# The last gate and routing ahead of the early experts, and the first batches' tables summed at the last scan's start

## The chip, the cores and the metric

One core of a Trainium2 chip runs the kernel. The metric is the device time in microseconds (us) of one execution; the kernel before took 2051.53 us, the median of three runs.

## The reference

The input x has 4 batches of 512 tokens of width 512. Four residual blocks follow each other. The last two are what the change is about: a state-space scan that is gated by the layer-normed x, and a mixture of experts over all 2048 tokens together.

```python
x = x + _L0_xattn_ref(_layernorm(x), fside, ctx)            # eight int8-quantised expert forwards
x = x + _L0_ffn_ref(_layernorm(x), lut, gate_idx, ...)      # dense FFN, weights looked up in a table of 16
x = x + _L1_xattn_ref(ctx, _layernorm(x), ...)              # scan over time, 512 channels x 16 states, times silu(z)
x = x + _L1_ffn_ref(_layernorm(x), gate_w, w_gate, w_up, w_down)   # mixture of experts
...
probs = softmax(x @ gate_w); w, sel = top_k(probs, 8); w = w / sum(w)
order = argsort(flat_e); pos = arange(P) - start[se]
slot = where(pos < C, se * C + pos, E * C)                  # C = 1024 slots for each of 32 experts
xg = x_pad[t_slot].reshape(E, C, H)
y = (silu(xg @ w_gate) * (xg @ w_up)) @ w_down
out = zeros((T + 1, H)).at[t_slot].add(w_slot[:, None] * y)
```

A token goes to 8 of 32 experts, and within an expert it takes the next free slot in token order. So an expert's list of slots needs the routing of all tokens that it is to work on.

## The kernel before

**Stages.** Weights of the second block are decoded first, woven with the first block. Then, for each batch b of 4, a scan (`scan`, lines 537 to 589) is woven with the second block's matmuls (`lut_ffn`), with `prepare` of the next batch, and with the gate and the routing of batch b-1. After the last scan, eight "early" experts (numbers 0 to 7) run over the tokens of batches 0 and 1. Then the PSUM banks are laid out anew, and 32 "late" expert calls follow: experts 8 to 31 over all tokens with 576 slots each, and experts 0 to 7 over batches 2 and 3 with 320 slots each. At the end two sums are added to x and written out.

**The order of the work.** The framework keeps a tile's buffers in pools. An instruction waits until its operands are there and until its output's buffer is free. Each engine runs its own instructions in a fixed order that follows the order of the program. `weave` takes steps of several generators in turn, in proportion to their given counts, and so sets that order; `chain` runs one generator after another, `run` runs one to its end. `pipeline` lets three experts overlap: while one is in its second matmul, the next is in its first, and the one after that is transposed.

**The scan.** For each of 64 groups of channels a tile `d` (tag "d", 4 buffers) is loaded by SP (L556). ScalarE makes the decay (`st`, L561), GpSimd the input term (`dBu`, L563), VectorE runs the recurrence (L566, L569), and TensorE sums over the states (`py`, L577). `BC` (L545) is loaded once for a batch. L587 ends each quarter of a scan.

**Gate and route.** `gate(b)` (L591 to L611) normalises x, multiplies with the scan's output, transposes (`pt_y`, L608), and adds to x. `route(b)` (L682 to L749) normalises x by blocks of 128 tokens (`xn_r`), stores these rows to DRAM (`xln`: one copy for the experts' gathers of batches 0 and 1, and one with all batches), transposes (`pt_r`), multiplies with the gate weights (`pl`, copied to `logits`), and takes the softmax and the best eight. `place` (L767 to L821) counts the tokens of each expert (`pp`), makes the slot numbers (`to`), and writes each token's number into its slot in a table in DRAM: 32 indirect DMAs of GpSimd for a batch (`table<-i_tok`, L814), which keep their order. There are two groups of eight tables: `tables[0]` for batches 0 and 1, `tables[1]` for 2 and 3. Within a group consecutive scatters go to different tables.

**Tables to tokens.** A slot is filled in one table of a group at most; the others hold zero there. `table_rows` (L823) loads the rows of several tables with one SP DMA for each (L835) into one tile `rows`, stacked over the partitions; with 24 experts, five tables fit on 128 partitions. `table_sum` (L841) adds the stacked tables by a matmul with a 0/1 matrix `pick` (L849 and L851 build it on VectorE from slices of the identity; L856 is the matmul). `slot_tokens` (L865) makes integer token numbers (for the gather) and row numbers (for the accumulate). The sums are named "a" (group 0, experts 0 to 7; read when the last scan begins), "u" (both groups, experts 8 to 31; read after the early experts) and "b" (group 1, experts 0 to 7; after "u").

**An expert** (`expert`, L896 to L990). SP loads its weights (`egu`, `ed`: 3 buffers each). GpSimd gathers its rows by indirect DMA (`xg`, L918, 10 buffers, blocks of 128; an early expert has 128, 128 and 64). TensorE transposes them (`pt_g`, L931), ScalarE and VectorE copy them (`exT`, L933), and ScalarE copies the routing weight of each row (`gates`, L934). Then come the first matmul (`pg`, L943), the activation (`eh`: tanh on ScalarE L959, two products on VectorE L960 and L961), the second matmul (`po_e`, L972 and L976), the scaling (`ey`, 4 buffers; VectorE L983 or ScalarE L985), and an indirect DMA of GpSimd which adds the rows to a sum in DRAM (`sums<-ey`, L986). An early expert's three blocks go to two sums in turn, so its third accumulate waits until its first has landed. PSUM banks of the early stage come under the tags "t" (two banks, shared by `pt_y`, `pt_r`, `pl`, `pp`, `pt_g`, `po_e` and the tables' sums), "m" and others.

Of the kernel before, what the change touches and what calls it, by code (L numbers as in the profile page):

```python
# [16 lines left out]
F32 = mybir.dt.float32  # L17
# [5 lines left out]
ALU = mybir.AluOpType  # L23
# [4 lines left out]
P = 128  # L28
NB = 4
S = 512  # L30
# [3 lines left out]
KH = HID // P  # L34
# [7 lines left out]
NE = 32  # L42
# [6 lines left out]
SLOTS = 576  # L49
EARLY = 8  # L50
ROOM = (320, 320)
# [8 lines left out]
class Kernel:  # L60
# [554 lines left out]
    def routing_constants(self, rp):  # L615
        nc, t = self.nc, self.t
        c = rp
        self.gate_w = c.tile([P, KH, NE], F32, name="gate_w", bufs=1)
        nc.sync.dma_start(out=self.gate_w, in_=t["gate_w"].rearrange("(k p) e -> p k e", p=P))
        tri = c.tile([P, P], F32, tag="xn", name="tri", bufs=1)  # L620
        make_upper_triangular(nc, tri, 1.0, diag=False)
        self.tri = c.tile([P, P], BF16, name="trib", bufs=1)
        nc.vector.tensor_copy(self.tri, tri)
        self.ones = c.tile([P, P], BF16, name="ones", bufs=1)
        nc.vector.memset(self.ones, 1.0)

        def iota(n, step, base, mult, name):
            i = c.tile([P, n], I32, name=f"{name}_i", bufs=1)
            nc.gpsimd.iota(i, pattern=[[step, n]], base=base, channel_multiplier=mult)
            f = c.tile([P, n], F32, name=name, bufs=1)  # L630
            nc.vector.tensor_copy(f, i)
            return f

        self.i_e = iota(NE, 1, 0, 0, "i_e")
        self.i_tok = iota(NT, P, 1, 1, "i_tok")
        row = iota(1, 0, 0, 1, "i_row")
        self.chosen = c.tile([P, NT, TOPK], F32, name="chosen", bufs=1)

        self.spare = c.tile([P, 2], F32, name="spare", bufs=1)
        nc.vector.tensor_scalar(self.spare[:, 0:1], row, float(NE * SLOTS), None, ALU.add)  # L640
        nc.vector.tensor_scalar(self.spare[:, 1:2], row, float(NE * CAP), None, ALU.add)
        self.no_row = c.tile([P, 1], F32, name="no_row", bufs=1)
        nc.vector.tensor_scalar(self.no_row, row, float(NB * S + 1), None, ALU.add)
        self.more_p = c.tile([P, 1], F32, name="more_p", bufs=1)
        nc.vector.memset(self.more_p, 0.0)
        self.seen = [c.tile([P, NE], BF16, name=f"seen{g}", bufs=1) for g in range(2)]
        for seen in self.seen:
            nc.vector.memset(seen, 0.0)
# [171 lines left out]
                self.tc.keep_in_program_order(scatter)  # L820
                yield  # L821

    def table_rows(self, pool, tag, tables, n, e0, e1, m):  # L823


        nc = self.nc
        ne = e1 - e0
        per = P // ne
        parts = -(-len(tables) // per)
        r = pool.tile([P, parts, m], F32, tag=tag, name="rows")  # L830
        rows = []
        for a in range(parts):
            group = tables[a * per : (a + 1) * per]
            for i, table in enumerate(group):
                nc.sync.dma_start(  # L835
                    out=r[i * ne : (i + 1) * ne, a, :],
                    in_=table[e0 * n : e1 * n].rearrange("(e n) o -> e (n o)", n=n)[:, :m],
                )
            rows.append(r[: len(group) * ne, a, :])
        return rows  # L840

    def table_sum(self, rp, rows, e0, e1, m, name):

        nc = self.nc
        nb = -(-m // P)
        ne = e1 - e0

        pick = rp.tile([P, ne], F32, tag="pick", name="pick", bufs=1)
        nc.vector.tensor_copy(pick, self.ident[:, :ne])  # L849
        for a in range(ne, P - ne + 1, ne):  # L850
            nc.vector.tensor_tensor(pick, pick, self.ident[:, a : a + ne], ALU.add)  # L851
        pt = self.bank("t", f"pt_{name}")
        for j in range(nb):
            w = min(P, m - j * P)
            for i, r in enumerate(rows):
                nc.tensor.matmul(  # L856
                    pt[:w, j * ne : (j + 1) * ne],
                    lhsT=r[:, j * P : j * P + w],
                    rhs=pick[: r.shape[0], :],
                    start=i == 0,  # L860
                    stop=i == len(rows) - 1,
                )
        return pt[:, : nb * ne].rearrange("p (j e) -> p j e", j=nb)

    def slot_tokens(self, rp, tok, m, name):  # L865

# [185 lines left out]
def run(steps):  # L1052
    for _ in steps:
        pass
# [15 lines left out]
def weave(*streams):  # L1070

    streams = [[0, n, g] for g, n in streams]
    while streams:
        s = min(streams, key=lambda s: s[0] / s[1])
        s[0] += 1
        if next(s[2], StopIteration) is StopIteration:
            streams.remove(s)
# [3 lines left out]
def tile_kernel(ctx: ExitStack, tc: tile.TileContext, t: dict):  # L1081
    k = Kernel(tc, t)
    k.constants(ctx)
    scan = ExitStack()
    with ExitStack() as early:
        with ExitStack() as ffn:
            wp = ffn.enter_context(tc.tile_pool(name="wp", bufs=1, side="right"))
            with ExitStack() as first:
                k.banks(first, t=2, m=2, y=2, d=2)
                ap = first.enter_context(tc.tile_pool(name="ap", bufs=2))  # L1090
                sq = staggered([k.smooth_quant(ap, b) for b in range(NB)], 15)
                with ExitStack() as lut:
                    lc = lut.enter_context(tc.tile_pool(name="lc", bufs=1, side="right"))
                    lp = lut.enter_context(tc.tile_pool(name="lp", bufs=2, side="right"))
                    k.lut_tables(lc, wp)
                    lookups = k.lut_weights(lp, k.jobs)
                    weave((islice(sq, 40), 40), (islice(lookups, 48), 48))
                    k.tile_rows(wp, lc)
                    weave((islice(sq, 48), 48), (lookups, 4 * len(k.jobs) - 48), (k.scratch(lc), 4 * CHAINS))

                pp = ffn.enter_context(tc.tile_pool(name="pp", bufs=1, side="right"))
                k.scan_weights(pp)
                k.prep_tag = "y"
                preps = 2 * KH + 1
                weave((k.prepare(pp, pp, 0), preps), (sq, 30 * NB - 88))
            k.banks(early, t=2, m=2, y=1, d=3)
            k.prep_tag = "t"
            bp = ffn.enter_context(tc.tile_pool(name="bp", bufs=2, side="right"))
            rp = ctx.enter_context(tc.tile_pool(name="rp", bufs=1))
            mp = scan.enter_context(tc.tile_pool(name="mp", bufs=2))  # L1110
            k.routing_constants(rp)
            steps = (TPB // 2) * (NIC + 3)
            units = KH * 16
            routes = TPB + 2 + TPB * TOPK

            ffn_ = chain(*(k.lut_ffn(bp, b) for b in range(NB)))
            run(islice(ffn_, 4))
            for b in range(NB):
                n = steps
                streams = [(k.scan(mp, b), units), (islice(ffn_, n), n)]  # L1120
                if b + 1 < NB:
                    streams.append((k.prepare(pp, (pp, mp)[(b + 1) % 2], b + 1), preps))
                if b:
                    run(k.gate(mp, b - 1))
                    streams.append((k.route(rp, b - 1), routes))
                if b == NB - 1:
                    rows = k.table_rows(rp, "xT", k.tables[0], SLOTS, 0, EARLY, ROOM[0])
                    tok = k.table_sum(rp, rows, 0, EARLY, ROOM[0], "a")
                    at = k.slot_tokens(rp, tok, ROOM[0], "a")
                weave(*streams)  # L1130
        ep = ctx.enter_context(tc.tile_pool(name="ep", bufs=2, side="right"))
        k.expert_buffers(ep)
        full, nc = SLOTS // P, tc.nc
        two = [k.sums[j % 2] for j in range(full + 1)]
        first = k.pipeline(k.expert(ep, e, (k.xln[0], *at, 0), e, ROOM[0], two) for e in range(EARLY))
        weave((chain(k.gate(mp, NB - 1), k.route(rp, NB - 1)), KH + routes), (first, 2 * EARLY))
    scan.close()
    k.banks(ctx, t=4, g=4)
    k.gu_tag = "g"
    tp = ctx.enter_context(tc.tile_pool(name="tp", bufs=6))  # L1140
    rows = k.table_rows(ep, "exT", k.tables[0] + k.tables[1], SLOTS, EARLY, NE, SLOTS)
    at = k.slot_tokens(rp, k.table_sum(rp, rows, EARLY, NE, SLOTS, "u"), SLOTS, "u")
    rows = k.table_rows(ep, "exT", k.tables[1], SLOTS, 0, EARLY, ROOM[1])
    at_b = k.slot_tokens(rp, k.table_sum(rp, rows, 0, EARLY, ROOM[1], "b"), ROOM[1], "b")
    k.overflow(rp)
    calls = [(e, at, e - EARLY, SLOTS) for e in range(EARLY, NE)]
# [64 lines left out]
```

## Time and profile before

| what | us |
|---|---|
| runs | 2049.74, 2051.53, 2053.53 |
| median of the runs | 2051.53 |
| the profiled execution's own time | 2053.26 |
| its span in the profile | 2051.4 |
| end of the last scan (L587) | 1162.0 |
| first early expert's `pt_g` | 1170.4 |
| last add of the last gate (L610) | 1193.7 |
| first and last scatter of the last batch (L814) start | 1237.2 and 1331.1 |
| last early expert's `po_e` ends | 1314.9 |
| first late expert's `pt_g` | 1349.6 |

The profile records one execution. All points of time in this document count from the start of its span. The engines are PE (TensorE matmul), PEld (TensorE's weight load, which overlaps), DVE (VectorE), ACT (ScalarE), POOL (GpSimd) and SP (SyncE, which issues DMAs; SPq is its queue). A timeline row gives start, duration, engine, line, operation, output<-inputs and shape; the bracket tells how long the engine was idle before it and what it waited for. A row of the waits gives the total, the number and the longest.

### The profile page before, as it was taken

What the parts mean: (1) busy time and instruction counts of PE and PEld (TensorE: products, weight loads), DVE (VectorE), ACT (ScalarE), POOL (GpSimd) and SP (SyncE); (2) the same over time, 40 slices, a digit from 0 to 9 for tenths busy, and PEclk for the clock granted to TensorE, in tenths of its full rate; (3) what the DMA queues carried; (4) which work ended last, traced back from release to release, by engine and by line L of the source; (5) the groups of instructions that cost most, each with busy time, mean ns of one, the idle gap of its engine ahead of it and who ended that gap; (6) DMA issues with size and microseconds to landing.
All of it is one profiled execution on the core that took longest, in us unless ns stands there. A gap on an engine that the chain in (4) does not pass through costs nothing. (4 is left out here: it accounts for less than half of the span.)

```text
span 2051.4 us, 24293 instructions
## 1 busy us (share of the span) xinstructions
PE 1681.2 (82%) x8385; PEld 991.7 (48%) x8385; DVE 1162.8 (57%) x1986; ACT 701.0 (34%) x1329; POOL 1113.8 (54%) x952
## 2 busy tenths in 40 slices
PE   4788774998887788787868679589999999999980
PEld 2444332655554455354636244265565565665640
DVE  6888764888788779776978533132222232322331
ACT  1554347345533544353423222122222222222210
POOL 3111015668557964697569726646565556555420
PEclk9989885999998998898989789889999999999995
DMA  9433613888777778586769666658888878778655
GB/s 266 122 108 107 221 32 102 209 201 220 196 178 178 187 190 215 132 210 169 204 140 234 172 177 145 130 147 189 179 195 177 191 154 188 166 159 183 124 129 180
DMA packets 193369, 348.97 MB, mean 170 GB/s; under 512 B 46370, under 2 KB 92930, under 8 KB 193236
## 3 DMA queue, kind: packets, MB, share of 16 engines
q1 hardware_dynamic: 148932, 254.19, 46.3%
q0 software_dynamic: 44048, 92.73, 23.1%
q8 instruction: 69, 1.13, 0.2%
q14 instruction: 64, 0.52, 0.1%
q10 hardware_dynamic: 256, 0.39, 0.1%
HBM read 278.12 MB, written 77.57 MB: 173 GB/s over the span
## 5 line engine op out<-in xcount | busy, mean ns | idle before, releaser
L943 PE MATMUL pg<-exT,egu 128*128 128x320 f32 (+1 forms) x1536 | 401.7, 419 | 12.3 <-DVE eh L960 7.9
L986 POOL DMA_INDIRECT sums<-ey,to x168 | 260.6, 1551 | 276.0 <-DMA sums<-ey,to 126.7
L563 POOL TENSOR_TENSOR dBu<-d,BC 128x512 f32<-128x512 f32 x256 | 324.6, 1280 | 81.3 <-DMA d<-dts 48.0
L943 PEld LDWEIGHTS pg<-exT,egu 128*128 128x128 f32 x1536 | 289.4, 192 | 130.2 <-issue 36.1
L569 DVE TENSOR_TENSOR_SCAN st<-st,dBu 128x512 f32<-128x512 f32 x192 | 231.2, 1219 | 107.6 <-POOL dBu L563 106.1
L561 ACT ACTIVATE st<-d,A 128x512 f32<-128x512 f32 x256 | 173.1, 688 | 268.7 <-DVE sc L570 207.3
L375 PE MATMUL pgu<-xT,wg 128*128 128x256 f32 (+1 forms) x704 | 193.8, 420 | 63.9 <-DVE h L385 56.1
L918 POOL DMA_INDIRECT xg<-xln,tokens x168 | 161.8, 963 | 112.3 <-PE pt_g L931 43.1
L375 PEld LDWEIGHTS pgu<-xT,wg 128*128 128x128 f32 (+1 forms) x704 | 135.5, 202 | 136.9 <-DVE h L385 73.6
L960 DVE SCALAR_TENSOR_TENSOR eh<-eh,pg 128x320 f32<-128x320 f32 (+5 forms) x144 | 61.1, 425 | 221.3 <-ACT eh L959 220.0
L340 PE MATMUL pw<-oh,lut_t 128*32 128x344 bf16 (+1 forms) x2052 | 127.9, 363 | 65.1 <-DVE oh L334 64.8
L972 PE MATMUL po_e<-ed,eh 128*128 128x512 f32 (+1 forms) x336 | 170.4, 627 | 10.8 <-ACT ey L985 6.3
L375 PE MATMUL pgu<-xT,wu 128*128 128x256 f32 (+1 forms) x704 | 174.2, 387 | 0.0
L983 DVE TENSOR_SCALAR ey<-po_e,gates 128x512 f32<-128x512 f32 x64 | 45.8, 747 | 217.6 <-PE po_e L976 207.6
L391 PE MATMUL po_f<-wd,h 128*128 128x512 f32 (+1 forms) x352 | 160.7, 611 | 8.9 <-DVE h L385 7.7
L985 ACT ACTIVATE ey<-po_e,gates 128x512 f32<-128x512 f32 (+1 forms) x104 | 68.8, 684 | 290.1 <-PE po_e L976 146.0
L814 POOL DMA_INDIRECT table<-i_tok,to x128 | 127.3, 995 | 42.3 <-issue 26.5
L375 PEld LDWEIGHTS pgu<-xT,wu 128*128 128x128 f32 (+1 forms) x704 | 135.8, 195 | 23.6 <-issue 1.9
L570 DVE TENSOR_TENSOR sc<-st,BC 128x512 f32<-128x512 f32 x192 | 126.5, 679 | 13.0 <-PE py L577 11.8
L567 POOL TENSOR_TENSOR sc<-sc,BC 128x512 f32<-128x512 f32 x64 | 82.0, 1282 | 90.4 <-DVE sc L566 49.7
L976 PE MATMUL po_e<-ed,eh 64*128 64x512 f32 (+1 forms) x336 | 114.3, 636 | 0.0
L391 PEld LDWEIGHTS po_f<-wd,h 128*128 128x128 f32 (+1 forms) x352 | 66.8, 194 | 96.4 <-issue 81.2
(268 smaller groups left out, 2225.0 us busy)
## 6 DMA issues: line engine op xcount, KB each, us to landing
d<-dts SPq DMA_DIRECT2D x256, 512.0 KB
egu<-in_w_gate SPq DMA_DIRECT2D x40, 384.0 KB
ix<-idx_b SPq DMA_DIRECT2D x16, 688.0 KB
egu<-in_w_up SPq DMA_DIRECT2D x40, 256.0 KB
ed<-in_w_down SPq DMA_DIRECT2D x40, 256.0 KB
ed<-in_w_down SPq DMA_DIRECT2D x80, 128.0 KB
sums<-zero SPq DMA_DIRECT2D x12, 768.0 KB
dts<-dt POOLq DMA_DIRECT2D x16, 512.0 KB, 4.6
```

What stands on the lines that cost most here:

```text
L340: nc.tensor.matmul(pt[i][32 * c : 32 * c + 32, :step], lhsT=self.lut_t[:, j, g, :], rhs=oh[:, c * n + i * step : c * n + (i + 1) * step], ...
L375: nc.tensor.matmul(pg[:m, j * W : (j + 1) * W], lhsT=w[:, k, c * P : c * P + m], rhs=xT[:, k, :], start=k == 0, stop=k == KH - 1,)
L391: nc.tensor.matmul(po, lhsT=h[:m, c, i * P : (i + 1) * P], rhs=self.wd[:m, c, :], start=c == 0, stop=c == NIC - 1,)
L561: nc.scalar.activation(st, d[:, 0, :], AF.Exp, scale=self.A[:, i : i + 1])
L563: nc.gpsimd.tensor_tensor(dBu, d[:, 1, :], BC[:, 0, :], ALU.mult)
L569: nc.vector.tensor_tensor_scan(st, st, dBu, 0.0, ALU.mult, ALU.add)
L570: nc.vector.tensor_tensor(sc, st, BC[:, 1, :], ALU.mult)
L814: scatter = nc.gpsimd.indirect_dma_start(out=tables[k % len(tables)], out_offset=bass.IndirectOffsetOnAxis(ap=to[:, i, k : k + 1], axis=0) ...
L918: nc.gpsimd.indirect_dma_start(out=xg[:m, :], out_offset=None, in_=xln, in_offset=bass.IndirectOffsetOnAxis(ap=tokens[:m, lo + j, col : co ...
L943: nc.tensor.matmul(pg[i][:, :hs], lhsT=w[:, k, i * P : (i + 1) * P], rhs=xT[:, k, z : z + hs], start=k == 0, stop=k == KH - 1,)
L972: nc.tensor.matmul(po[j][:m, :], lhsT=h[:, 0, b : b + m], rhs=wd[:, 0, :], start=True, stop=False)
L986: nc.gpsimd.indirect_dma_start(out=sums[j], out_offset=bass.IndirectOffsetOnAxis(ap=to[:m, lo + j, col : col + 1], axis=0), in_=y[:m, :], ...
```

## The change

1. The `pick` matrices (for 8 and for 24 experts) are built once, in the routing's constants, and kept.
2. When the last scan begins, after the sum "a", the rows of `tables[0]` for experts 8 to 31 are read as well. Their eight loads go into two tiles of the scan's tag "d" (five tables in one, three in the other). They are summed at once, and the sum is copied to a tile `known`.
3. After the scans, the last gate and the last route are issued whole, and after them the early experts; before, the two were woven.
4. After the early experts only the eight tables of `tables[1]` are loaded for the sum "u", by SP and ScalarE in turn; `known` is added to their sum. The rows of "b" are also loaded by both in turn.

```diff
@@ routing_constants
+        self.picks = {}
+        for ne in (EARLY, NE - EARLY):
+            self.pick(c, ne)
@@ table_rows
-    def table_rows(self, pool, tag, tables, n, e0, e1, m):
+    def table_rows(self, pool, tag, tables, n, e0, e1, m, queues=False, r=None):
...
-                nc.sync.dma_start(
+                issue = nc.scalar if queues and i % 2 else nc.sync
+                issue.dma_start(
@@ new
+    def pick(self, rp, ne):
+        if ne not in self.picks:
+            nc = self.nc
+            pick = self.picks[ne] = rp.tile([P, ne], F32, name=f"pick{ne}", bufs=1)
+            nc.vector.tensor_copy(pick, self.ident[:, :ne])
+            for a in range(ne, P - ne + 1, ne):
+                nc.vector.tensor_tensor(pick, pick, self.ident[:, a : a + ne], ALU.add)
+        return self.picks[ne]
@@ table_sum
-        pick = rp.tile([P, ne], F32, tag="pick", name="pick", bufs=1)
-        nc.vector.tensor_copy(pick, self.ident[:, :ne])
-        for a in range(ne, P - ne + 1, ne):
-            nc.vector.tensor_tensor(pick, pick, self.ident[:, a : a + ne], ALU.add)
+        pick = self.pick(rp, ne)
@@ new
+    def add_tokens(self, rp, tok, other, m, name):
+        nc = self.nc
+        out = rp.tile(list(tok.shape), F32, tag=f"tok_{name}", name="tok", bufs=1)
+        for a, z, w in ((0, m // P, P), (m // P, -(-m // P), m % P)):
+            if a == z:
+                continue
+            if other is None:
+                nc.vector.tensor_copy(out[:w, a:z, :], tok[:w, a:z, :])
+            else:
+                nc.vector.tensor_tensor(out[:w, a:z, :], tok[:w, a:z, :], other[:w, a:z, :], ALU.add)
+        return out
@@ tile_kernel
                     at = k.slot_tokens(rp, tok, ROOM[0], "a")
+                    rows = []
+                    for group in (k.tables[0][:5], k.tables[0][5:]):
+                        r = mp.tile([P, 2, S], F32, tag="d", name="rows", bufs=4)
+                        r = r.rearrange("p a s -> p (a s)").unsqueeze(1)[:, :, :SLOTS]
+                        rows += k.table_rows(mp, "d", group, SLOTS, EARLY, NE, SLOTS, r=r)
+                    tok = k.table_sum(rp, rows, EARLY, NE, SLOTS, "u")
+                    known = k.add_tokens(rp, tok, None, SLOTS, "known")
                 weave(*streams)
...
-        weave((chain(k.gate(mp, NB - 1), k.route(rp, NB - 1)), KH + routes), (first, 2 * EARLY))
+
+        run(chain(k.gate(mp, NB - 1), k.route(rp, NB - 1)))
+        run(first)
...
-    rows = k.table_rows(ep, "exT", k.tables[0] + k.tables[1], SLOTS, EARLY, NE, SLOTS)
-    at = k.slot_tokens(rp, k.table_sum(rp, rows, EARLY, NE, SLOTS, "u"), SLOTS, "u")
-    rows = k.table_rows(ep, "exT", k.tables[1], SLOTS, 0, EARLY, ROOM[1])
+    rows = k.table_rows(ep, "exT", k.tables[1], SLOTS, EARLY, NE, SLOTS, True)
+    tok = k.add_tokens(rp, k.table_sum(rp, rows, EARLY, NE, SLOTS, "u"), known, SLOTS, "u")
+    at = k.slot_tokens(rp, tok, SLOTS, "u")
+    rows = k.table_rows(ep, "exT", k.tables[1], SLOTS, 0, EARLY, ROOM[1], True)
```

In the changed program's order this stands on the engines: on PE the last gate's transposes, the route's transposes and logits, then the experts; on GpSimd the gathers of the first experts, all 32 scatters of the last batch, and then the accumulates of the early experts; on ScalarE nine `gates` copies of the first experts still stand ahead of the route's first `xn_r`.

More of the change, by code (lines that the diff above doesn't have):

```diff
@@ L829, in table_rows @@
         parts = -(-len(tables) // per)
-        r = pool.tile([P, parts, m], F32, tag=tag, name="rows")
+        if r is None:
+            r = pool.tile([P, parts, m], F32, tag=tag, name="rows")
         rows = []
```

## The prediction

> **What bounds the kernel now.** I read the page first (engine shares and slices), then a table of windows over three stretches, then the waits of the stretch that the change touches, then its timelines. From the page:
>
> ```profile
> PE 1681.2 (82%) x8385; PEld 991.7 (48%) x8385; DVE 1162.8 (57%) x1986; ACT 701.0 (34%) x1329; POOL 1113.8 (54%) x952
> PE   4788774998887788787868679589999999999980
> PEclk9989885999998998898989789889999999999995
> ```
>
> The reader is to see that TensorE carries the second half, at nine tenths and more, and that there is one dip before it (slices 24 to 26, 51.3 us each). The windows (us, then busy us of PE, PEld, DVE, ACT, POOL, then clock, DMA share, GB/s) cut at the end of the last scan and at the first late expert:
>
> ```profile
> 0.00:1162.00 1162.00, 907.56 (x5386) 528.78 (x5386) 905.27 (x1460) 496.04 (x793) 659.21 (x583) 0.90 0.66 172
> 1162.00:1350.00 188.00, 136.50 (x505) 79.72 (x506) 53.84 (x153) 39.50 (x99) 96.57 (x86) 0.83 0.66 155
> 1350.00:2052.00 702.00, 637.09 (x2496) 383.17 (x2494) 203.67 (x376) 165.45 (x438) 357.98 (x284) 0.95 0.76 170
> ```
>
> In the middle stretch PE has 136.5 us of work in 188. It is a chain: eight early experts, the 32 table scatters of the last batch, the tables' sum, the first late gather. The waits of 1314 to 1350 and three timelines (start, duration, what, idle before and releaser) name its links:
>
> ```profile
> PE pt_u L856 <- DMA rows<-table: 17.8, 2, 15.0
> POOL xg L918 <- DVE to_f L877: 12.6, 1, 12.6
> PE pt_b L856 <- DVE pick L851: 4.2, 1, 4.2
> ...
> 1313.85 1.07 PE L976 MATMUL po_e<-ed,eh 64*64 64x512 f32 x2
> 1335.94 8.13 PE L856 MATMUL pt_u<-pick,rows 120*128 120x24 f32 x36 [14.98 <-DMA rows<-table]
> ...
> 1237.17 0.99 POOL L814 DMA_INDIRECT table<-i_tok,to  x1 [1.25 <-DVE to L811]
> 1331.14 0.98 POOL L814 DMA_INDIRECT table<-i_tok,to  x1 [0.30 <-issue]
> 1344.70 1.00 POOL L918 DMA_INDIRECT xg<-xln,tokens  x1 [12.57 <-DVE to_f L877]
> ```
>
> The experts end at 1314.9, but the last scatter starts only at 1331.1, and the late experts at 1349.6 (first pt_g): a gap of 34.7 us with PE nearly idle. It can be had only if the scatters go sooner and the experts don't end later by as much.
>
> [...] scatters and accumulates start in program order. [...] granted clock 0.50 in 1320 to 1340, and four transposes take 1.11 us cold, 0.60 warm. [...] scatters here land in 2.1 us (median of 1200 to 1340), accumulates in 4.5. [...]
>
> **The change, part by part.**
>
> *Pick matrices once* (21 small VectorE operations near 360 us for 16+5+16 later). Early, 5 more of about 0.16 us on an engine with slack: nothing. Late, pt_b's 4.2 us wait for pick goes, but the first late gathers land only at about 1348.2 (gather 1344.7 plus 3.5), so it was beside them: nothing.
>
> *First tables summed at the last scan's start.* Eight loads of 54 KB from SP, two of the scan's four d buffers, 20 passes of pt_u. PE: 20 x 0.2 = 4 us at about 988, where PE waits 0.96 and 3.1 us at 990.5 and 997.4: hidden, otherwise 4. The buffers are the doubt. SP's timeline has three d loads at 961.3 and one at 966.3, ahead of BC's two (969.8); now BC comes first, the first two d loads find buffers, and the third and fourth wait for pt_u, which stands after pt_a (987.7) and is through at about 992. POOL idles 7.8 us there until 988.7, as it is. d loads in the steady scan come 2.45 us apart, so I take one load behind: +2.4, bounds 0 and +6 (the two loads and BC's delay); a much greater loss is rival B.
>
> *Last gate and route first.* Now the last-batch gate's sixteen transposes and four adds stand ahead of the experts: the adds ended at 1193.7, now with only the gate's own work at about 1169.8 (L587 ends at 1162.0, then tanh, product, transposes, adds: 7.8). But ScalarE has nine gates copies (L934, for the experts' first nine gathers) ahead of the first normalise xn_r in its queue. Before, the ninth ran at 1180.9; the gathers are still issued first by POOL, 1.27 apart, so xn_r starts at about 1181 (bound: 1177.2, if only ln_rs behind ten gathers decides).
>
> Each of route's four rounds took 4.6 us (xn_r at 1199.6 and 1213.4: 13.8 for three), bound by xn's one buffer and its stores, with 4.86 from last xn_r to logits. So logits end at 1181 + 13.8 + 4.9 = 1199.7 (before 1218.3). Logits to mask was 7.7, of which 1.0 was experts' copies: 6.7, so 1206.4. pp to the indices 9.0, less 1.8 of experts' VectorE work: 7.2, plus 0.5 to POOL: first scatter S = 1214.1 (before 1237.2). Route thus gains 23, not the 32 its place suggests.
>
> Thirty-two scatters now stand together on POOL: 32 x 1.273 = 40.7, done at 1254.8 instead of 1332.1. Queued behind them are all accumulates of the experts. ey has 4 buffers, an expert uses 3, so e0 and one block of e1 are written, and then PE cannot go on: e1's po_e waits for ey, e2's eh for ScalarE's ey, e3's pt_g for the PSUM bank. By about S+28 all that can run has run. What releases it is the first accumulate's landing. From 1254.8: landing 5.7 (the trace's accumulates have 3.7 to 5.9), second accumulate 1.9, ey 0.7, tanh and products of e2 2.3, its third pg 2.4, eh 0.6, pt_g of e3 1.6, po_e of e2 5.2: e3's pg starts at 1275.2, plus 1.5 for a cold PE. It was 1244.02. From there to the end of e7 the trace has 70.84 (14.2 per expert, with scatters between; POOL then needs about 9.4 per expert, so it doesn't bound): T = 1347.5, against 1314.9. So +32.6.
>
> *The gap after it.* Only the second tables' rows are left, landed by 1260 and read while e6 and e7 run. After T: ey 0.8, pt_u 20 passes of 0.2 = 4.0, adding `known` and tokens 1.2, first gather at T+6.0, landed and copied 3.5 later: pt_g at T+9.6 = 1357.1. The gap is 9.6 instead of 34.7: -25.1. ScalarE's queue for three of the eight loads costs 3 issues in e6/e7: nothing, since ScalarE was 21% busy there (39.5 of 188).
>
> *Warmth.* PE comes to the late experts after a shorter idle stretch: the first 20 transposes took 4.26 at half clock and take 2.30 warm: -2 (0 to -2).
>
> Sum: +32.6 - 25.1 - 2.0 + 2.4 = +7.9. The late experts are the same instructions in nearly the same order. The profiled execution took 2053.3 (span 2051.4, so 1.9 around it); 2053.3 + 7.9 = 2061.2. That execution was 1.7 above the median of the runs shown, so on the median's footing 2059.5.
>
> **Rivals.** 0.2% is 4.1 us, about what a measurement of this kernel can tell from no change.
>
> (A) The sum above, slower by 4 to 13: 2055.6 to 2064.5. It follows if POOL's scatters really stand as one block with accumulates behind. Chance 0.48.
>
> (B) The scan starves: two of four d buffers are gone while its pipeline fills, pt_u is itself behind the late scatters of batch 2, and every j of the first rounds waits for a load: +5 to +12 on top of (A), the middle of it 2059.5 + 8 = about 2067. For it: DMA is at 0.8 to 0.9 in 1000 to 1150, so a lost start isn't made good; against: POOL idles there anyway, and VectorE is only 81% busy. Chance 0.12.
>
> (C) Even: the experts' stall is shorter than I make it (S at about 1207, or the experts from e3 on need 13.2 instead of 14.2 each with no scatter between, which is -5 to -7): 2047.4 to 2055.6, about 2051.5. Chance 0.18.
>
> (D) The other side, faster: the route, no longer sharing ScalarE, VectorE and PSUM banks with experts, runs at the bound of its stores. With xn_r from 1177.2 and rounds of 3.0 (0.8 normalise, 2.1 landing as for a late scatter) logits end at 1191, S is 1205, T falls by 9; with no loss in the scan and -2 warm the sum is 2051.5 - 4 = 2047.5. It decides from S at or below about 1205. For it: xn_r's rounds contain waits of 1.3 to 2 us for PE, which experts cause in part. Against: ScalarE's gates copies stand ahead, and in the trace xn_r's releaser was the store. Chance 0.22.
>
> **How the numbers follow.** Likeliest is (A), 2059.5, its own range 2055.6 to 2064.5. Range for 8 in 10: down to 2045 takes in C and D, up to 2068 most of B. Faster by over 0.2%: 0.22 (D); within: 0.18 (C); slower: 0.60 (A and B).
>
> **What would show it.** In the profile after: the ninth gates copy before xn_r at about 1181; 32 scatters in one row from about 1214, 1.27 apart; PE idle about 20 us before e2's po_e with the sums' landing as releaser; e7's last po_e at about 1347; first late pt_g under 10 us behind it; no row of pt_u waiting 15 us. Wrong if S is before 1205, if the experts from e3 on take under 13 us each, or if the last scan ends other than 0 to 6 us later than 1162.

## The result

The changed kernel takes 2068.34 us (median of 5 runs, 2067.94 to 2075.07) against 2052.41 (5 runs) for the kernel before: 1.0074 times as long, 95% interval 1.0046 to 1.0101: 16 us slower between the medians, 15 by the ratio.

The profiled execution of the changed kernel is its slowest run, 2075.07 us (span 2073.3), 6.7 above its median; that of before was within 1 us of its own. So 21.9 us between the two spans have to be told from about 16 between the medians. The page of the changed kernel (engine shares, then tenths busy in 40 slices):

```profile
PE 1691.8 (82%) x8376; PEld 999.6 (48%) x8385; DVE 1164.3 (56%) x1974; ACT 701.8 (34%) x1329; POOL 1114.1 (54%) x952
PE   4788765999787779787868475989999999999980
PEclk9989985999998898898989678989999999999995
```

The work is the same. The one low slice of before (a 5 in slice 26) has become two, a 4 in slice 23 (1140 to 1192 us) and a 5 in slice 25 (1244 to 1296). To see where the time went, I counted each stretch from an event that both kernels have: D, the issue of the last `dts` store of batch 3 (L535 on POOL) just before the last scan, and G, the first gather of the early experts.

| stretch, us | before | after | difference |
|---|---|---|---|
| start of the span to D | 970.05 | 972.25 | +2.2 |
| D to G: the last scan and the gate's normalise | 192.73 | 199.38 | +6.65 |
| G to the end of e7's po_e: route and early experts | 152.14 | 184.06 | +31.9 |
| e7's end to the first late pt_g: the gap | 34.71 | 9.07 | -25.6 |
| first late pt_g to the end | 701.77 | 708.54 | +6.8 |

PE's timeline of the changed kernel (start, duration, what, idle before and releaser):

```profile
1249.46 4.57 PE L968 MATMUL pg<-exT,egu 128*128 128x320 f32 x16
1267.94 0.47 PE L956 MATMUL pt_g<-ident,xg 128*128 128x128 f32 x1 [13.91 <-DVE ey L1008]
1273.44 4.03 PE L968 MATMUL pg<-exT,egu 128*128 128x320 f32 x8 [5.03 <-issue]
1284.84 4.57 PE L968 MATMUL pg<-exT,egu 128*128 128x320 f32 x16
...
1354.62 1.07 PE L1001 MATMUL po_e<-ed,eh 64*64 64x512 f32 x2
1356.47 2.31 PE L868 MATMUL pt_u<-pick,rows 120*128 120x24 f32 x20 [0.77 <-ACT ey L1010]
1364.76 1.11 PE L956 MATMUL pt_g<-ident,xg 128*128 128x128 f32 x4 [4.62 <-DMA xg<-xln,tokens]
```

The third `pg` of e2 starts only at 1273.4, 19.4 us after the first two have ended, and e3 follows at 1284.8. The 15 us wait for the rows is gone, and pt_u is down to 20 passes. POOL's timeline and the waits of 1160 to 1400 (total, times, longest) name what stood between:

```profile
1221.47 1.01 POOL L817 DMA_INDIRECT table<-i_tok,to  x1 [0.60 <-DVE to L814]
1261.02 0.97 POOL L817 DMA_INDIRECT table<-i_tok,to  x1 [0.30 <-issue]
1262.30 1.62 POOL L1011 DMA_INDIRECT sums<-ey,to  x1 [0.30 <-issue]
...
1359.60 1.44 POOL L1011 DMA_INDIRECT sums<-ey,to  x1 [2.31 <-DMA ed<-in_w_down]
1361.34 1.02 POOL L943 DMA_INDIRECT xg<-xln,tokens  x1 [0.30 <-issue]
```

```profile
ACT ey L1010 <- DMA sums<-ey,to: 26.6, 2, 21.8
DVE ey L1008 <- DMA sums<-ey,to: 23.6, 1, 23.6
```

Thirty-two scatters stand in one block of 40.5 us, and the first accumulates right behind it. Until these have landed, VectorE stands 23.6 us ahead of its `ey` and ScalarE 21.8. PE's products for the two had been there since 1246.7 and 1249.5, so some 20 us of either are the wait for a buffer.

**The last scan.** The second loss is before all this. SP, POOL, PE and VectorE at the scan's start, first in the kernel before, then in the changed one:

```profile
961.34 1.87 SPq L556 DMA_DIRECT2D d<-dts  x3
966.30 0.51 SPq L556 DMA_DIRECT2D d<-dts  x1
969.80 1.16 SPq L546 DMA_DIRECT2D BC<-xdbl  x2
970.05 0.65 POOL L535 DMA_DIRECT2D dts<-dt  x1 [0.30 <-POOL dt L534]
973.38 5.10 POOL L563 TENSOR_TENSOR dBu<-d,BC 128x512 f32<-128x512 f32 x4 [2.68 <-DMA BC<-xdbl]
```

```profile
963.11 4.20 SPq L840 DMA_DIRECT2D rows<-table  x10
972.03 1.16 SPq L546 DMA_DIRECT2D BC<-xdbl  x2
973.29 15.46 SPq L556 DMA_DIRECT2D d<-dts  x5
982.02 0.52 SPq L556 DMA_DIRECT2D d<-dts  x1
983.70 0.52 SPq L556 DMA_DIRECT2D d<-dts  x1
972.25 0.65 POOL L535 DMA_DIRECT2D dts<-dt  x1 [0.30 <-POOL dt L534]
980.25 1.74 POOL L563 TENSOR_TENSOR dBu<-d,BC 128x512 f32<-128x512 f32 x1 [7.35 <-DMA d<-dts]
982.37 1.31 POOL L563 TENSOR_TENSOR dBu<-d,BC 128x512 f32<-128x512 f32 x1 [0.37 <-DMA d<-dts]
986.95 1.27 POOL L563 TENSOR_TENSOR dBu<-d,BC 128x512 f32<-128x512 f32 x1 [3.27 <-DVE sz L602]
993.54 4.17 PE L868 MATMUL pt_u<-pick,rows 120*128 120x24 f32 x20 [0.84 <-DVE x L610]
997.75 0.26 DVE L885 COPY tok<-pt_u 128x96 f32<-128x96 f32 x1 [3.27 <-PE pt_u L868]
1003.04 1.27 POOL L563 TENSOR_TENSOR dBu<-d,BC 128x512 f32<-128x512 f32 x1 [7.50 <-DVE ln_rs L103]
```

Before, four `d` tiles had been issued when BC came, and POOL made four inputs in a row, 3.3 us after D. Now BC's loads keep their place beside D, but the d loads are issued behind them, and POOL stands 7.35 us until the first has landed. With the rows in two of the four d buffers, the third and the fourth load (rows 982.02 and 983.70, two of the five) go only when POOL has read the first and the second tile. The third input then starts at 986.95; its row names VectorE, but its load landed at 986.81, 0.14 us ahead. Then VectorE, which runs the recurrence, waits 3.27 us at the copy of the sum that pt_u is making, with the scan's next step queued further behind it; POOL waits 7.5 us in turn. Against the kernel before, the 9th input after D is 7.8 us late, the 16th 6.9 (55.2 against 48.3), the 29th 3.9 (103.3 against 99.4): about half of the loss at the start is made good later.

### The profile page after: what moved, and what is told of

Its sections match the earlier page's. It is cut to its first block, busy times and chain, and to the rows that moved or that the text cites. A ratio compares the mean times of both kernels' runs of the same rounds, so it can differ in the third digit from the quotient of the medians.

```text
span 2073.3 us, 24266 instructions
## 1 busy us (share of the span) xinstructions
PE 1691.8 (82%) x8376; PEld 999.6 (48%) x8385; DVE 1164.3 (56%) x1974; ACT 701.8 (34%) x1329; POOL 1114.1 (54%) x952
## 5 line engine op out<-in xcount | busy, mean ns | idle before, releaser
L563 POOL TENSOR_TENSOR dBu<-d,BC 128x512 f32<-128x512 f32 x256 | 325.0, 1281 | 103.3 <-DMA d<-dts 59.1
L561 ACT ACTIVATE st<-d,A 128x512 f32<-128x512 f32 x256 | 173.4, 689 | 266.7 <-DVE sc L570 196.6
L375 PE MATMUL pgu<-xT,wg 128*128 128x256 f32 (+1 forms) x704 | 199.9, 430 | 63.0 <-DVE h L385 55.2
L375 PEld LDWEIGHTS pgu<-xT,wg 128*128 128x128 f32 (+1 forms) x704 | 140.4, 209 | 135.9 <-DVE h L385 72.2
```

The source lines that it names most:

```text
L375: nc.tensor.matmul(pg[:m, j * W : (j + 1) * W], lhsT=w[:, k, c * P : c * P + m], rhs=xT[:, k, :], start=k == 0, stop=k == KH - 1,)
L561: nc.scalar.activation(st, d[:, 0, :], AF.Exp, scale=self.A[:, i : i + 1])
L563: nc.gpsimd.tensor_tensor(dBu, d[:, 1, :], BC[:, 0, :], ALU.mult)
```

## The experiments

The runs were made in three series of four, each on one chip, the three on different chips, where the kernel before has medians of 2066.6, 2066.5 and 2059.6 us. Each ratio is to the kernel before in the same series; "middle" is the stretch from G to the first late pt_g in the profile (186.85 before, 193.13 changed).

**1. The order and the early sum taken apart.** The first kernel keeps the old weave and all else of the change:

```diff
-        run(chain(k.gate(mp, NB - 1), k.route(rp, NB - 1)))
-        run(first)
+        weave((chain(k.gate(mp, NB - 1), k.route(rp, NB - 1)), KH + routes), (first, 2 * EARLY))
```

> The changed kernel with gate, route and early experts woven as before; the early sum, the single pick matrices and the two queues stay. Theory (two losses, 6.6 us in the last scan and some 6 to 8 behind it from the order): the scan's 6.6 stays, the order's loss goes, and the late pt_u has 20 passes instead of 40 (4 us less): first gather of the early experts about 1169, last scatter about 1338, first late pt_g about 1352; time 2052.4 + 2.5 = about 2055. Rival (the order is the whole loss, the scan's shift only drift between executions): first gather at 1163 to 1165, time 2052.4 - 4 = about 2048. Rival (the early sum is the whole loss): time as the changed kernel, about 2068.

Measured: 1.0026 (1.0012 to 1.0039), +5 us by the ratio. D to G took 197.27, so the scan's loss is there without the new order; the middle took 185.88, only 1 us less than before. The second is the kernel before with the new order alone (the same two lines the other way round):

> The kernel before with the last gate and route ahead of the early experts, nothing else: all sixteen tables summed after the early experts, pick built each time. Theory: the scan isn't delayed (first gather about 1163), e7's last po_e ends about 1347 as in the changed kernel less its scan's shift, then 40 passes (4 us more than 20): first late pt_g about 1360; time 2052.4 + 10 to 12 = about 2063. Rival (the loss is all in the scan): 2052 to 2054.

Measured: 1.0121 (1.0098 to 1.0143), +25 us: twice what the theory said. D to G was 193.41, without a loss in the scan, as expected, but the middle took 211.8. The size is taken up in 3.

**2. The scatters woven with the experts.** Gate and route run first only up to the slot positions:

```diff
-        run(chain(k.gate(mp, NB - 1), k.route(rp, NB - 1)))
-        run(first)
+        last = chain(k.gate(mp, NB - 1), k.route(rp, NB - 1))
+        run(islice(last, KH + TPB + 2))
+        weave((last, 2 * TPB * TOPK), (first, 2 * EARLY))
```

> The changed kernel, but gate and route run first only as far as the slot positions; the 32 scatters are then woven with the early experts, all within the first half of the experts' steps. Theory (the block of 32 scatters ahead of the accumulates stalls PE for 21 us between e2 and e3): no such stall, e3's pg about 21 us earlier (1264), first late pt_g about 1344, time 2068.3 - 21 = about 2047. Rival (PE waits for the late start of the experts and for weights or gathers, not for the accumulates): e3's pg still beyond 1275, time 2063 to 2068.

Measured: 0.9997 (0.9982 to 1.0011), no change against before, where the changed kernel is 1.0074. First scatter 49.85 us after G as in the changed kernel (49.84), e7's end at 177.2 and the middle 186.5. The experts start as late as in the changed kernel, and the loss is gone: without the block the late start is just paid back by the shorter gap. But the 21 us of the theory weren't reached: e3's first pg came at 1275.4, 9.5 us earlier than in the changed kernel, and not at 1264. With scatters in between, e0 and e1 take 20 and 21 us and e2 to e4 15.4, against 14.35 without; POOL's work is spread, not gone.

**3. The early sum out of the scan.** The eight loads, the twenty passes and the copy are issued after the last gate, from the same d buffers, which the scan no longer needs then (in the diff the eight lines are cut to their first and last):

```diff
@@ at the last scan's start
-                    rows = []
...
-                    known = k.add_tokens(rp, tok, None, SLOTS, "known")
@@ after the last scan
-        run(chain(k.gate(mp, NB - 1), k.route(rp, NB - 1)))
+        run(k.gate(mp, NB - 1))
+        rows = []
...
+        known = k.add_tokens(rp, tok, None, SLOTS, "known")
+        run(k.route(rp, NB - 1))
         run(first)
```

> The changed kernel with its early sum (eight loads into two d buffers, twenty passes) issued after the last gate instead of at the last scan's start, where no scan load competes. Theory (the eight loads and two buffers at the scan's start cost the scan 6.6 us): first gather about 1165, the sum hidden while ScalarE waits for the gathers, time 2068.3 - 6.6 = about 2062. Rival (the shift of the scan was drift between executions): about 2068.

Measured: 1.0071 (1.0046 to 1.0095), as slow as the changed kernel had been, where 1.003 was expected. Yet in the profile D to G took 193.43: the scan's loss was gone, and the middle took 209.35. The sum isn't free here either: the first scatter came 51.93 us after G, 2.1 later than in the changed kernel. Both kernels with the block of scatters in this series had a middle some 16 to 19 us longer than the changed kernel's first profile. I ran the kernel before and the changed one again, side by side:

> The kernel before, unaltered, for a profile beside the others of this series. Theory (the 13 and 18 us of idle ScalarE in the early experts of the last two profiles come with the block of 32 scatters): none of that here; from the issue of the last dts store to the first gather 192.7 us, from the first gather to the first late pt_g 186.9 us, each within 2. Rival (the idle comes with the chip): the second interval is 195 or more here too.

> The changed kernel, unaltered, beside the others of this series. Expected: 1.007 times the kernel before; from the last dts store to the first gather 4 to 7 us longer than before (the early sum at the scan's start), from the first gather to the first late pt_g 6 us longer (the order). Rival (the order costs more where ScalarE is held up under the scatters): the second interval 15 us longer or more, ratio 1.012.

The kernel before: middle 186.47, as its theory had it (the rival's 195 is out); D to G 195.41, 2.7 more than in its first profile and so past the 2 that were allowed. The changed kernel: middle 206.19, D to G 197.24, ratio 1.0086 (1.0062 to 1.0109). Here the order costs 20 us in the profile and not 6, as the rival had it; the ratio's interval holds 1.007 and not the rival's 1.012. The profiled run is the slowest of its six, 7 us above their median. ScalarE's timeline of this second profile of the changed kernel:

```profile
1242.47 0.38 ACT L959 COPY gates<-xg 128x1 f32<-128x1 f32 x3
1255.09 0.27 ACT L984 ACTIVATE eh<-pg 64x128 f32<-64x128 f32 x1 [12.23 <-remote]
1256.03 0.32 ACT L984 ACTIVATE eh<-pg 64x192 f32<-64x192 f32 x1 [0.67 <-issue]
1272.60 0.44 ACT L984 ACTIVATE eh<-pg 128x320 f32<-128x320 f32 x1 [16.25 <-remote]
```

In the program this tanh waits for PE alone, and PE's records show the operands made by 1243.4. It starts 12 us later, and its third part 16 us after the second, 11 after the recorded end of its operands (1261.4), for nothing that the profile names ("remote"). In the first profile of the changed kernel the same three ran 1.3, 0.7 and 0.9 us apart. So here e1, not e2, is the last expert to get on before the scatters end, and one expert more (14.35 us) is left for afterwards. The same stands in the profiles of 1's second kernel and of 3: ahead of e1's third pg PE is idle for 16.0 and 14.0 us with no releaser, and for 13.7 here. What holds ScalarE there is open. Shorter waits without a releaser stand in three more profiles of these two chips (7.8 us in that of the kernel before, 6.0 in that of 2 and 3 together, 4.2 in that of 2), and none stands in the first pair or on the third series' chip. So the chip is a rival to the block of scatters as what brings them, and no run here parts the two.

With 2 and 3 in one kernel:

> The last two edits together: gate and route first, scatters woven with the experts, and the early sum after the last gate. Theory (two separate losses, each taken away by its edit): scan not delayed, no stall between e2 and e3: the woven one's 0.9997 less 4.5 us, ratio 0.9975. Rival (taking the sum out of the scan brings nothing, as the ratio of 1.0071 with it suggested): 0.9997.

Measured: 0.9989 (0.9972 to 1.0007); D to G 193.84, middle 185.67. The interval holds both 0.9975 and 0.9997, so the time decides nothing; the profile shows the scan's stretch shorter by 3 us than in 2 (196.86).

Taken over all profiles, the scan's loss is plain. The first input after D came at 7.9 to 8.1 us in all five profiles with the early sum at the scan's start, and at 3.3 to 4.2 in the nine others; the 29th at 102.7 to 103.8, and at 96.5 to 99.9. D to G was 196.6 to 199.4 in the five, and 190.2 to 195.4 in the others; the means differ by 4.4 us.

**4. What the experts wait for.** The changed kernel with more buffers for ey:

```diff
-                y = ep.tile([P, HID], F32, tag="ey", name="ey", bufs=4)
+                y = ep.tile([P, HID], F32, tag="ey", name="ey", bufs=12)
```

> The changed kernel with twelve instead of four buffers for ey, nothing else. Theory (the early experts stand because ey's buffers come free only with the accumulates behind the 32 scatters): four experts can run through the scatters, e7's last po_e ends 14 to 18 us earlier counted from the first gather (about 168 instead of 184 to 197), ratio 0.999 to 1.001. Rival (ScalarE is held up while POOL issues scatters, whatever buffers there are): idle of 12 us and more before tanh stays, ratio 1.005 or more.

Measured: 1.0038 (1.002 to 1.0055), between the two. Whether that is a gain over the changed kernel's 1.0074 and 1.0086 can't be told, since the changed kernel was not run on this chip, and the profile shows none: e7 ended 184.20 us after G, to 0.2 us as in the first profile of the changed kernel; the theory's 168 is missed. No idle time without a releaser is in this profile, so the rival isn't it either. ScalarE and PE in this kernel:

```profile
1245.49 0.19 ACT L959 COPY gates<-xg 128x1 f32<-128x1 f32 x1
1265.91 0.52 ACT L959 COPY gates<-xg 128x1 f32<-128x1 f32 x2 [20.23 <-DMA xg<-xln,tokens]
```

```profile
1249.08 0.27 PE L956 MATMUL pt_g<-ident,xg 128*128 128x128 f32 x1
1268.46 4.14 PE L968 MATMUL pg<-exT,egu 128*128 128x320 f32 x8 [19.11 <-issue]
```

With buffers to spare ScalarE goes on to the gates copies of e4, whose second and third gathers are behind the scatters on POOL too (1261.2 and 1262.6, the last scatter being at 1256.2), and e2's tanh is queued behind these copies. The stall has the same place and length with another releaser. So it isn't the buffers alone that hold the experts: whatever of theirs comes behind the block on POOL does.

**5. The other way: keep the weave, and let the scatters go sooner.** The nominal number of steps for gate and route sets how fast `weave` advances them. First this number alone, in the kernel before:

```diff
-        weave((chain(k.gate(mp, NB - 1), k.route(rp, NB - 1)), KH + routes), (first, 2 * EARLY))
+        weave((chain(k.gate(mp, NB - 1), k.route(rp, NB - 1)), 60), (first, 2 * EARLY))
```

> The kernel before with 60 instead of 42 nominal steps for gate and route in the weave, nothing else: all sixteen tables are read and summed after the early experts. Theory (half of the gain of 0.9929 comes from the earlier scatters, half from the 20 passes and the pick matrices that no longer stand in the gap): first late pt_g at 185 to 186 us from the first gather, ratio 0.998. Rival (the order of the scatters is all): 0.993. Rival (it is nothing): 1.000.

Measured: 0.9974 (0.9957 to 0.999), 5 us faster than before with one number changed, as the theory had it; the middle, 182.9, is 2 to 3 us shorter than forecast. Then with the early sum after the last gate, the single picks and the two queues, and the number at 42 (as before), 60 and 84. The one of 60 was run first, in the second series, and so on another chip than the rest of this section; here its edit:

```diff
+        def early_sum():
...
+            known.append(k.add_tokens(rp, tok, None, SLOTS, "known"))
+            yield
-        run(chain(k.gate(mp, NB - 1), k.route(rp, NB - 1)))
-        run(first)
+        last = chain(k.gate(mp, NB - 1), early_sum(), k.route(rp, NB - 1))
+        weave((last, 60), (first, 2 * EARLY))
```

> The version with 60 steps, with the 42 of before: the early sum after the last gate, single picks, two queues, the old weave. Theory (the scan's loss is gone against the first experiment, 1.0026 less 4.5 us; the last scatter still goes after e7): ratio 1.0004, first late pt_g 184 to 186 us from the first gather. Rival (the 60 steps bring nothing, the later sum all): 0.993.

> Gate, route and experts woven as before, but with 60 instead of 42 nominal steps for gate and route, so that the last scatter goes when 11 of the experts' 16 steps are issued; the early sum after the last gate. Theory (POOL's work behind the first scatter, 98 us of scatters, accumulates and gathers, sets the end of the early stage; with the scatters ahead in it the last accumulates run while the tables are read): first late pt_g about 9 us earlier than before, ratio 0.9955. Rival (each scatter put ahead delays an accumulate and the experts by as much): 0.999 to 1.001.

> The version with 60 steps, with 84: the last scatter goes when 8 of the experts' 16 steps are issued. Theory (POOL's work behind the first scatter sets the end; with 60 the scatters are out of the way already): no further gain, ratio 0.991 to 0.995. Rival (the denser the scatters, the more accumulates wait, as in the changed kernel): 0.997 to 1.003.

| steps | ratio | last scatter, e7's end, first late pt_g (us after G) |
|---|---|---|
| before (42) | 1 | 168.4, 152.1, 186.9 |
| 60 alone | 0.9974 (0.9957 to 0.999) | 144.8, 168.5, 182.9 |
| early sum later, 42 | 0.9996 (0.9977 to 1.0015) | 171.6, 163.9, 186.2 |
| early sum later, 60 | 0.9929 (0.9902 to 0.9957) | 155.2, 168.3, 181.0 |
| early sum later, 84 | 1.0007 (0.9988 to 1.0026) | 135.9, 171.1, 181.9 |

Of the three, 42 came as its theory had it (the middle 0.2 us past its range), and its rival, that the later sum does it all, is out. 60 is faster than its theory's 0.9955, though its middle is only 5.5 us shorter than that of the kernel before on its chip, where 9 were forecast. 84 missed its theory (0.991 to 0.995) and lies in its rival's range. The version of 42 differs from experiment 1's first kernel (1.0026) in where the early sum stands, and its 0.9996 is a second sign of the scan's loss, in the timed runs: some 6 us, on two chips, with intervals that just overlap.

With 60 the last scatter goes before e7 ends. POOL and PE at the end of the early stage, with 60 alone:

```profile
1308.09 0.96 POOL L814 DMA_INDIRECT table<-i_tok,to  x1 [0.30 <-issue]
1340.89 1.44 POOL L986 DMA_INDIRECT sums<-ey,to  x1 [4.84 <-DMA sums<-ey,to]
1342.64 1.01 POOL L918 DMA_INDIRECT xg<-xln,tokens  x1 [0.30 <-DVE pick L851]
```

```profile
1332.49 7.04 PE L856 MATMUL pt_u<-pick,rows 120*128 120x24 f32 x40 [0.77 <-ACT ey L985]
1346.17 1.12 PE L931 MATMUL pt_g<-ident,xg 128*128 128x128 f32 x4 [0.96 <-DMA xg<-xln,tokens]
```

All 40 passes end at 1339.5, and the first late gather still goes only at 1342.6, right behind e7's third accumulate, which itself waits 4.84 us for the first one's landing. The same two rows follow each other in the changed kernel (1359.60 and 1361.34 above; there the accumulate stood 2.31 us). So once the scatters are out of the way, 20 passes fewer seem to gain little: the middle is 182.9 with 40 and 181.0 with 20, in one profile each, on two chips.

The two versions that beat both kernels are the one of 60 alone (18 runs) and the one of 60 with the early sum after the gate (0.9929, 6 runs on one chip). Of the second's 11 us between medians its profile shows 5.5 in the middle; the version of 84 has nearly the same middle and isn't faster. So its time is less well founded than its interval looks, and 0.9974 for the number alone is the safer finding.

## Why the prediction was half right

It forecast slower, by 8 us on the median's footing; it is 15 to 16. Counted from the 2051.53 that it started from, its range went up to +16.5, so the change lies at the range's upper end, and above the likeliest case's own range (+4 to +13).

**Right, by their own terms.** The order: first scatter 49.84 us after G (1214.1 less 1162.8 gives 51.3); the block of scatters 40.5 (40.7); e3's first pg 113.2 after G (113.9 for 1276.7); e7's end +31.9 (+32.6); the gap -25.6 (-25.1), itself 9.07 (9.6). The order's net, +6.3 from G to the first late pt_g, was forecast as +7.5, though the second profile of the changed kernel has 20 there. The chain that was named for the release (accumulate, landing, ey, tanh) is what this profile shows. The prediction's estimate of 1.5 us for a cold PE was near: the eight passes of pg behind the wait took 4.03 us at a granted clock of 0.58, 1.6 more than the same eight of e3 (2.39 at 1.00). The pick matrices cost and gained nothing that a profile shows.

**Right in number, for a wrong reason: route's rounds.** The prediction took 4.6 us for a round, "bound by xn's one buffer and its stores". Without experts in between the rounds still take 4.7 (the first xn_r at 1188.58, the fourth at 1202.76), but each starts right behind the logits copy of the round before, on ScalarE:

```profile
1193.19 0.19 ACT L718 COPY logits<-pl 128x32 f32<-128x32 f32 x1 [2.00 <-PE pl L711]
1193.27 0.81 ACT L111 ACTIVATE xn_r<-x,ln_off,ln_rs 128x512 f32<-128x512 f32 x1
```

No store is waited for. ScalarE's own order, with its waits for PE inside a round, sets the pace, and that, not the store, is what kept rival D's rounds of 3.0 away in this profile. That the two reasons give the same number was luck.

**Mis-sized: the last scan.** "One load behind: +2.4, bounds 0 and +6" measured +6.65 in this pair of profiles, and 4.4 between the means of the five profiles with the early sum at the scan's start and of the nine without it. The prediction saw that BC would come first and that two buffers would be gone, but priced them at one load and left the rest to its upper bound; the first input came about 4 us later in every profile of the five. Its own sign of being wrong here came: the last scan ended at 1170.8 and not 0 to 6 us behind 1162.0, 2.2 of the 8.8 being there ahead of D. It let the third and fourth load wait for pt_u; they waited for POOL to read the first two. And it put the 4 us of pt_u into PE's idle time and left out VectorE's copy, which waits for pt_u (1.4 to 3.3 us) on the engine that the scan needs. Rival B, a scan that starves at its start, gave about 2067: the time measured is nearly its own, and its first rounds that wait for loads are what POOL's timeline shows; I had given it 0.12. Its number is met in part by luck: it had the scan lose 5 to 12 us beyond the 2.4, and no pair of profiles of one comparison shows so much.

**Not found: warmth.** I took -2 for a warmer start of the late experts; that a shorter idle stretch ahead of them would leave the clock up was my estimate, and no trace had shown it. The first four transposes took 1.1 us in both kernels, at a granted clock of 0.50 in both, and in the changed one, where PE had been idle for 4.62 us just before, they waited for one gather after another. In the kernel before the 20 transposes ran in a row, since the first gather had been issued 4.9 us ahead of them; now they start 3.4 us behind it and meet each gather as it lands. The wait for pick had covered that. From the first late pt_g to the first po_e it is 19.6 us against 17.3 in this pair, so +2.3; in the second series' pair it is 19.7 against 23.7, where the kernel before has a wait of 7.8 us without a releaser, so the sign is not settled.

**Probably not from the change.** The remaining 4.4 us in the late experts and the 2.2 ahead of D: in the other profiles, from the first late pt_g to the end took 704.6 to 716.1, and D came at 969.7 to 977.5, and in the second series' pair, on one chip, the late part is 711.9 before and 711.8 changed. The sum by steps from the first two profiles is then +6.65 (scan), +6.3 (order) and +2.3 (start of the late experts), 15.3, near the medians' 16; one pair of profiles doesn't make that split firm.

**Not foreseen.** In the first two series the order cost 20 us and more in the profiles (experiment 3), with waits that have no releaser. The ratio there, 1.0086, and the first one, 1.0074, overlap; how much of it is in the timed runs of the first comparison can't be told from their one profile. The timed runs give the order a larger part than the first profile does: 1.0026 with the old weave against 1.0074 and 1.0086 with the new order, each on its own chip, is 10 to 12 us.

## What to carry to other kernels

Count what a step moved ahead puts into each engine's order, and read off what is behind it there: 32 transfers of 1.27 us in one block on GpSimd held the accumulates and gathers behind them (in all five profiles with the block the first accumulate started 1.3 us after the last scatter), and more buffers only changed the name of ScalarE's wait (21.8 us for a landing with four, 20.2 for a gather with twelve). A sum taken early isn't free merely because its engine is idle: the instruction that reads the result waited as well, on its own engine (VectorE, 1.4 to 3.3 us here). When two streams share an engine, try the proportion of the weave before the order: here one number (60 for 42) gave 5 us, where the order alone cost 25, and a larger one (84, with the later sum) gave nothing.

## What was not expected of the hardware

In three of the five profiles in which the 32 scatters stand in one block, PE was idle ahead of e1's third pg for 13.7 to 16.0 us with no releaser (16.0 in the kernel with the order alone, 14.0 in the one with the sum after the gate, 13.7 in the changed one's second profile, where ScalarE's tanh started 12 and 11 us after the recorded ends of PE's passes), and not in the two others (the changed one's first profile, and that with twelve ey buffers). The three belong to the first and second series, on two chips, where shorter waits without a releaser, of 4.2 to 7.8 us, stand in woven orders as well; the two others belong to the first comparison and the third series. No row of the profile names a cause, and it wasn't settled.
